# A graph layer with attention and experts: where the last node tiles' work stands in the queues

## The chip, the cores and the metric

The kernel runs on one core of a Trainium2 chip. The metric is the device time of one execution in microseconds (us). Each number of "time" is a median of several executions; the profile is one execution, taken by the hardware profiler.

## The reference

The input is 6250 nodes of 256 features and 206,250 directed edges (src, dst). With `xn = layernorm(x)` the layer computes three things.

```
# 1. graph attention, 4 heads of 64 features
h  = xn @ W;  el = h @ Wl.T;  er = h @ Wr.T
e  = exp(leaky_relu(el[src] + er[dst], 0.2))          # one weight per edge and head
g  = elu(segment_sum(e * h[dst], src) / segment_sum(e, src) + b)
# 2. linear attention with 4 memory entries, 4 heads of 32
q, k, v = split(rmsnorm(xn) @ w_qkv)
q = softmax(q over the features of a head);  k = softmax(k over all nodes)
a = rmsnorm(((k.T @ v) applied to q) @ w_out + b_out) + xn
# 3. mixture of 8 experts, the best 2 of each node
x2 = x + g + a
t  = layernorm(x2)
y  = t + sum over experts of combine[:, e] * (gelu(t @ w1[e] + b1[e]) @ w2[e] + b2[e])
out = x2 + y
```

## The kernel before

**Tiles.** The nodes lie in 49 tiles of 128 (the last one has 106). The edges are 1612 columns of 128.

**Sorting and projecting.** Four node tiles at a time are normalised and multiplied with all weights of the first two parts (`project`); the rows that the edges will need go to a table in DRAM. Between these groups, and behind them, `sort_batch` runs 51 times. It takes 32 columns of edges and puts them in order of their pairs of node tiles: a one-hot `ob` (L381), counts `n_ps` (L389) and their scan `inc` (L393), the sums `ahead` (L406), the ranks' sums `r_ps` in PSUM (matmuls L413 and L414), `rank` from them (L421 and L427), `rank2` on ACT (L433), the values `rv` (L438), the one-hot `ohp` (L442), and 32 matmuls into `g_ps` (L448), which ACT copies to `grid` (L453). Pool `sps` has one buffer of each PSUM tile; `rv` and `ohp` have two. `context` computes the keys' softmax and `k.T @ v` between the last batches.

**Packing and gathering.** `pack(q)` makes from the grid the ordered list of edges of two node tiles (on DVE the products `rc` L914 and one-hots `ohc` L907, `ohp` L919; on PE `s_ps` L924). For each of the two tiles `gather` then issues 35 indirect DMAs on GpSimd's queue (POOL, L952). Each brings 128 rows of 69 numbers into one column of `xe`, of which there are three buffers.

**Node tiles.** The loop at L1051 goes over blocks of up to GT = 4 node tiles. A node tile `b` does `weights` (scores `z`: the reduction L998, the addition L1002, which is the first to need the gathered rows; the exponential L1005; the copy L1006) and then four times `sums` (the product `ohw` on DVE, L1014, and some 24 matmuls into `a_ps`, L1021), `look` for the next tile (its one-hots and `e_ps`), in odd tiles a `pack`, and `some_more`. ACT then copies the sums (`a_s`, L1067), PE transposes them (L1070), and `heads` divides by the weights' sums (L817 to L819).

**What is done beside it.** `todo` is a queue of generators. The first is `attention`: three steps for each of 13 groups, 39 in all. Each finished block adds `finish_steps`: `front` (elu, sum and layernorm, L665 to L709), `route` (the best two experts, L712 to L757), and nine steps over the experts, in each of which `hidden` computes one expert's two halves (`h_ps` L764, Gelu L772) and `result` adds the expert before it (`y_ps` L780, `x` L784); 11 steps in all. `hps` has one buffer, so `h_ps` is one PSUM bank. When the attention has ended, the experts' weights are loaded (`open_experts`). `some_more()` runs one step; `some_more(c)` runs the c-th part of what is still in the queue. In blocks of four each quarter of a tile calls it once; in smaller blocks the queue is spread over the quarters that are left in the block. The 49 tiles are cut into nine blocks of four and then 3, 2, 2, 2, 1, 1, 1, 1, which end at tiles 38, 40, 42, 44, 45, 46, 47 and 48.

**Order.** The framework puts the instructions of each engine in an order of its own from the order written down, its estimates of when operands are there, and the dependencies; on the chip each engine then runs its queue in that order. A `NoSync` dependency fixes an order on one engine and waits for nothing. `keep_in_program_order` ties an instruction behind the one written just before it on its engine. Should more edges than there are columns belong to a tile, `flag` is set and a slow path recomputes everything.

Of the kernel before, what the change touches and what calls it, by code (L numbers as in the profile page):

```python
# [17 lines left out]
P = 128  # L18
GT = 4
# [16 lines left out]
def tile_gps_layer(  # L36
# [43 lines left out]
    NB = NQ + NQ % 2  # L80
    BB = min(CB, 512 // NB)
    assert BW % BB == 0 and U == 2
    TW = H + FO + 1
    VW = HF + H
    CS = CPT // S
# [6 lines left out]

    groups = [(t0, min(GT, NT - t0)) for t0 in range(0, NT, GT)]

    sizes = []
    while sum(sizes) < NT:
        sizes.append(min(GT, -(-(NT - sum(sizes)) // (GT + 1))))
    blocks = [(sum(sizes[:i]), n) for i, n in enumerate(sizes)]

    cp = ctx.enter_context(tc.tile_pool(name="const", bufs=1))  # L100
# [263 lines left out]
    def sort_batch(t):  # L364
# [41 lines left out]
        nc.vector.tensor_tensor(  # L406
            pairs(ahead[:, :w]), two(inc[:, :w], NB // 2), row(delta, NB // 2), op=OP.mult
        )
        r_ps = sps.tile([P, BW // BB, 512], F32, name="r_ps")
        for i, a in enumerate(range(0, w, BB)):  # L410
            z = min(w, a + BB)
            part = r_ps[:, i, :(z - a) * NB]
# [20 lines left out]
        nc.scalar.activation(  # L433
            rank2[:, :w], rank[:, :w, None].to_broadcast([P, w, 2]), AF.Identity, bias=less_own
        )
        rv = sw.tile([P, BW, 2, NB], F16, name="rv")
        for i, v in enumerate((va, vb)):
            nc.vector.tensor_tensor(  # L438
                pairs(rv[:, :w, i, :]), pairs(ob[:, :w]), two(v[:, cs], NB // 2), op=OP.mult
            )  # L440
        ohp = sw.tile([P, BW, P], F16, name="ohp")
        nc.vector.tensor_tensor(  # L442
            pairs(ohp[:, :w]), two(rank2[:, :w], P // 2), row(iota_h, P // 2), op=OP.is_equal
        )
# [206 lines left out]
        W["fw"] = fx.enter_context(tc.tile_pool(name="ffnw", bufs=1, side="right"))  # L651


    def finish_steps(hps, yps, x2, t0, n, rows_left, gb):

        w = n * P
        held = {}
# [101 lines left out]
        def hidden(e, f):  # L759
            if f == 0:  # L760
                held[e] = fw.tile([P, FC, GT * P], F32, name="hT", bufs=2)
            h_ps = hps.tile([P, GT * P], F32, name="h_ps")
            for c in range(DC):
                nc.tensor.matmul(  # L764
                    h_ps[:, :w],
                    lhsT=w1s[:, e, c, f * P:(f + 1) * P],
                    rhs=held["tokT"][:, c, :w],
                    start=(c == 0),
                    stop=(c == DC - 1),
                )  # L770
            k = e * FC + f
            nc.scalar.activation(  # L772
                held[e][:, f, :w], h_ps[:, :w], AF.Gelu, bias=b1s[:, k:k + 1]
            )

        def result(e, js):
            for j in js:
                y_ps = yps.tile([P, D], F32, name="y_ps")
                for f in range(FC):
                    nc.tensor.matmul(  # L780
                        y_ps, lhsT=held[e][:, f, j * P:(j + 1) * P], rhs=w2s[:, e, f, :],
                        start=(f == 0), stop=(f == FC - 1),
                    )
                nc.vector.scalar_tensor_tensor(  # L784
                    x2[:, j, :], y_ps, held["comb"][:, j, e:e + 1], x2[:, j, :],
                    op0=OP.mult, op1=OP.add,
                )

        def store():
            full = n if rows_left is None else n - 1  # L790
# [69 lines left out]
    def pack(q):  # L860
# [88 lines left out]
    def gather(dst_x):  # L949
        xe = gw.tile([P, CPT, TW], F32, name="xe", bufs=3)  # L950
        for c in range(CPT):
            nc.gpsimd.indirect_dma_start(  # L952
                out=xe[:, c, :],
                out_offset=None,
                in_=table,
                in_offset=bass.IndirectOffsetOnAxis(ap=dst_x[:, c:c + 1], axis=0),
            )
        return xe
# [34 lines left out]
                    start=False, stop=(g0 + g == GC - 1),  # L993
                )

    def weights(xe, e_ps):
        z = gw.tile([P, CPT, H], F32, name="z")
        nc.vector.tensor_reduce(  # L998
            z, e_ps[:, 1:].rearrange("p c i h -> p c h i"), axis=AX.X, op=OP.add
        )  # L1000

        tc.keep_in_program_order(nc.vector.tensor_add(z, z, xe[:, :, :H]))  # L1002
        nc.vector.scalar_tensor_tensor(z, z, 0.2, z, op0=OP.mult, op1=OP.max)
        ew = gw.tile([P, CPT, H], F32, name="ew")
        nc.scalar.activation(ew, z, AF.Exp)  # L1005
        nc.vector.tensor_copy(ew_s, ew)  # L1006


    def sums(i, oh, xe, a_ps):
        g0, g1 = CELLS[i]  # L1010
        n = g1 - g0
        c0 = i * CS - 1 + g0
        ohw = gw.tile([P, GC, H, SN], F32, name="ohw")
        nc.vector.tensor_tensor(  # L1014
            ohw[:, :n],
            oh[:, g0:g1, i, None, :].to_broadcast([P, n, H, SN]),
            ew_s[:, c0:c0 + n, :, None].to_broadcast([P, n, H, SN]),
            op=OP.mult,
        )
        for c in range(c0, c0 + n):  # L1020
            nc.tensor.matmul(  # L1021
                a_ps[:, i].rearrange("f h n -> f (h n)"),
                lhsT=xe[:, c, H:],
                rhs=ohw[:, c - c0].rearrange("p h n -> p (h n)"),
                start=(c == c0), stop=(c == c0 + n - 1),
            )
# [24 lines left out]
    for t0, n in blocks:  # L1051
        x2 = gw.tile([P, GT, D], F32, name="x2", bufs=3)
        for j in range(n):
            b = t0 + j
            xe, _ = ready.pop(b)
            oh, e_ps = seen.pop(b)
            weights(xe, e_ps)
            a_ps = pa.tile([FO + 1, S, H, SN], F32, name="a_ps")
            for k in range(S):
                sums(k, oh, xe, a_ps)  # L1060
# [13 lines left out]
            heads(x2[:, j, :], hd_ps[:, :, :FO], hd_ps[:, :, FO])  # L1074
        rows_left = None if (t0 + n) * P <= N else last
        todo.append([finish_steps(hps, yps, x2, t0, n, rows_left, gb_s), NX + 3])

    seen_n = count[0:1].rearrange("p q u s -> p (q u) s")[:, :NT]
    away = cp.tile([1, NT, S], F32, name="away")
# [137 lines left out]
```

## Time and profile before

| what | before |
|---|---|
| time, median of 3 runs | 2762.55 us (2759.88 to 2763.56) |
| time of the profiled execution | 2760.09 us |
| its span, first to last instruction | 2758.0 us |
| mean granted TensorE clock | 0.82 |
| busy: PE, DVE, ACT, POOL | 76%, 70%, 27%, 61% |
| first gather issued, last gather's end | 443.9 us, 2635.4 us |

PE is TensorE's matmuls, PEld its weight loads, DVE VectorE, ACT ScalarE, POOL GpSimd, SP the queue of plain transfers. A row of a group reads: line, engine, operation, what it writes and reads, how often, then the busy time in us, the mean duration in ns, and the time that its engine stood idle just before it with what ended that. A row of waits reads: who waited for whom, us in total, times, longest. A row of stretches reads: from and to, length, busy time of each engine with its number of instructions, granted clock, share of the DMA engines, GB/s. A line of the timeline reads: start, duration, engine, line and operation, and in brackets the idle time before it and what ended it. All in us from the start of the span.

### The profile page before, as it was taken

The page shows a single profiled execution, that of the slowest core. Times are in us where ns is not written, and L with a number is a line of the kernel's source. Part 1 is how long each engine was busy: PE and PEld are TensorE (multiplying, and loading weights), DVE is VectorE, ACT ScalarE, POOL GpSimd, SP SyncE. Part 2 cuts the span into 40 slices and gives each one's busy share as a digit, 9 for nine tenths or more (in the row PEclk, how much of TensorE's full clock was granted, in tenths as well). Part 3 has the DMA queues.
Part 4 walks back from the last instruction along what each step waited for, and adds up shares of the span by engine and source line. Part 5 has one row for each costly group of instructions (what it writes and reads, how often), then busy time and mean ns, then how long its engine had stood idle before and what let it go on. Part 6 is the DMA issues. An engine that isn't in the chain of part 4 may idle for free.

```text
span 2758.0 us, 39898 instructions
## 1 busy us (share of the span) xinstructions
PE 2108.4 (76%) x15539; PEld 1584.8 (57%) x15539; DVE 1939.9 (70%) x3992; ACT 753.6 (27%) x1691; POOL 1688.5 (61%) x1779
## 2 busy tenths in 40 slices
PE   6888664556465498969899889596895988887987
PEld 3555442445354367656667667465675666666774
DVE  6877977668487668775879568765776676876742
ACT  4655311112231132213223222021221322232333
POOL 1000204777777777777677777777777777777610
PEclk9878665666677599979999889698796999888887
DMA  2110200222222422121212212212122221221110
GB/s 70 33 30 25 20 1 15 44 59 58 58 59 52 109 36 44 29 44 29 41 29 44 37 36 37 36 29 36 36 29 36 34 40 29 38 37 34 33 15 5
DMA packets 106775, 103.96 MB, mean 38 GB/s; under 512 B 42822, under 2 KB 78884, under 8 KB 106580
## 3 DMA queue, kind: packets, MB, share of 16 engines
q0 software_dynamic: 54880, 60.70, 14.6%
q1 hardware_dynamic: 50004, 39.75, 5.1%
q8 instruction: 124, 2.03, 0.3%
q10 hardware_dynamic: 1696, 0.89, 0.1%
q14 instruction: 71, 0.58, 0.1%
HBM read 86.57 MB, written 14.65 MB: 37 GB/s over the span
## 4 chain that ended last, share of the span: by engine, by line
POOL 29%; PE 26%; DVE 15%; issue 14%; ACT 2%; DMA 2%; DVEq 0%; ACTq 0%; POOLq 0%
POOL xe L952 28%; PE a_ps L1021 8%; PE h_ps L764 7%; PE y_ps L780 6%; DVE rc L914 4%; DVE ohp L919 3%; DVE ohc L907 2%; DMA xe<-table,dst_x 2%; PE y_ps L704 1%; DVE ohw L1014 1%; PE y_ps L755 1%; PE s_ps L924 1%; DVE x L784 1%; POOL kv L492 1%; PE y_ps L699 1%
## 5 line engine op out<-in xcount | busy, mean ns | idle before, releaser
L952 POOL DMA_INDIRECT xe<-table,dst_x x1715 | 1654.5, 965 | 632.7 <-issue 604.4
L1021 PE MATMUL a_ps<-ohw,xe 128*65 128x128 f32 x4410 | 552.1, 283 | 16.3 <-DVE ohw L1014 12.7
L1021 PEld LDWEIGHTS a_ps<-ohw,xe 128*65 128x65 f32 x4410 | 518.2, 144 | 50.9 <-DVE ohw L1014 19.2
L924 PE MATMUL s_ps<-rc,ohp 128*128 128x144 f16 x2525 | 257.4, 275 | 279.7 <-DVE ohp L919 279.6
L764 PE MATMUL h_ps<-tokT,w1s 128*128 128x512 f32 (+3 forms) x1088 | 431.3, 515 | 47.5 <-ACT hT L772 45.4
L924 PEld LDWEIGHTS <-ohp 128*128 128x128 f16 x2525 | 224.7, 121 | 342.9 <-DVE ohp L919 321.5
L780 PE MATMUL y_ps<-w2s,hT 128*128 128x256 f32 x1568 | 405.6, 390 | 0.0
L784 DVE SCALAR_TENSOR_TENSOR x<-y_ps,comb,x 128x256 f32<-128x256 f32 x392 | 189.0, 484 | 230.3 <-PE y_ps L780 230.0
L1014 DVE TENSOR_TENSOR ohw<-oh,bank 128x1280 f32<-128x1280 bf16 x196 | 323.4, 1650 | 32.3 <-PE a_ps L1021 30.8
L780 PEld LDWEIGHTS y_ps<-w2s,hT 128*128 128x128 f32 x1568 | 285.0, 193 | 66.3 <-issue 28.7
L772 ACT ACTIVATE hT<-h_ps,b1s 128x512 f32<-128x512 f32 (+3 forms) x272 | 154.4, 568 | 555.4 <-PE h_ps L764 412.1
L764 PEld LDWEIGHTS h_ps<-tokT,w1s 128*128 128x128 f32 x1088 | 193.6, 205 | 151.3 <-ACT hT L772 79.5
L914 DVE TENSOR_TENSOR rc<-ohc,bank 128x1152 f16<-128x1152 f16 (+1 forms) x350 | 228.0, 693 | 4.5 <-PE s_ps L924 0.7
L919 DVE TENSOR_TENSOR ohp<-to,bank 128x2048 f16<-128x2048 f16 (+1 forms) x175 | 195.1, 1115 | 0.0
L981 ACT COPY ohT<-t_ps 128x768 bf16<-128x768 bf16 x98 | 78.2, 798 | 319.0 <-PE t_ps L977 318.9
L1002 DVE TENSOR_TENSOR z<-z,xe 128x140 f32<-128x140 f32 x49 | 15.0, 307 | 210.6 <-DMA xe<-table,dst_x 202.5
L350 POOL COPY el<-tab 128x16 f32<-128x16 f32 (+1 forms) x13 | 3.5, 267 | 260.7 <-ACT tab L349 260.7
L907 DVE TENSOR_TENSOR ohc<-to,bank 128x1152 f16<-128x1152 f16 (+1 forms) x175 | 121.2, 692 | 0.4 <-ACT to L896 0.4
L442 DVE TENSOR_TENSOR ohp<-rank,iota_h 128x4096 f16<-128x4096 f16 (+1 forms) x51 | 116.1, 2277 | 6.3 <-ACT rank L433 6.0
L342 PE MATMUL pr<-wcat,xT 128*128 128x456 f32 x196 | 109.9, 691 | 5.9 <-ACT xT L339 5.9
L1067 ACT COPY a_s<-a_ps 65x512 f32<-65x512 f32 x49 | 28.4, 580 | 280.6 <-PE a_ps L1021 280.4
L448 PEld LDWEIGHTS <-ohp 128*128 128x128 f16 x1612 | 62.3, 109 | 56.4 <-DVE ohp L442 45.6
(269 smaller groups left out, 2483.9 us busy)
## 6 DMA issues: line engine op xcount, KB each, us to landing
xe<-table,dst_x POOLq DMA_INDIRECT x1715, 2.5
xt<-in_x_dram SPq DMA_DIRECT2D x24, 512.0 KB, 3.9
base_y<-xt SPq DMA_DIRECT2D x12, 512.0 KB
yt<-base_y SPq DMA_DIRECT2D x9, 512.0 KB, 4.4
out_dram<-x SPq DMA_DIRECT2D x9, 512.0 KB
w1s<-in_L_ffn_w_dram SPq DMA_DIRECT2D x8, 256.0 KB
w2s<-in_L_ffn_w_dram SPq DMA_DIRECT2D x8, 256.0 KB, 5.3
table<-tab SPq DMA_DIRECT2D x12, 138.0 KB
```

What stands on the lines that cost most here:

```text
L442: nc.vector.tensor_tensor(pairs(ohp[:, :w]), two(rank2[:, :w], P // 2), row(iota_h, P // 2), op=OP.is_equal)
L764: nc.tensor.matmul(h_ps[:, :w], lhsT=w1s[:, e, c, f * P:(f + 1) * P], rhs=held["tokT"][:, c, :w], start=(c == 0), stop=(c == DC - 1),)
L772: nc.scalar.activation(held[e][:, f, :w], h_ps[:, :w], AF.Gelu, bias=b1s[:, k:k + 1])
L780: nc.tensor.matmul(y_ps, lhsT=held[e][:, f, j * P:(j + 1) * P], rhs=w2s[:, e, f, :], start=(f == 0), stop=(f == FC - 1),)
L784: nc.vector.scalar_tensor_tensor(x2[:, j, :], y_ps, held["comb"][:, j, e:e + 1], x2[:, j, :], op0=OP.mult, op1=OP.add,)
L907: nc.vector.tensor_tensor(pairs(ohc[:, :m]), twos(to[:, 0, t0:t0 + m], U * CW // 2), iota_2[:, :, :U * CW // 2].to_broadcast([P, m, U * CW ...
L914: nc.vector.tensor_tensor(pairs(rc[:, :m, i, :]), pairs(ohc[:, :m]), twos(edges_q[:, t0:t0 + m, i, :], U * CW // 2), op=OP.mult,)
L919: nc.vector.tensor_tensor(pairs(ohp[:, :m]), twos(to[:, 1, t0:t0 + m], P // 2), iota_2.to_broadcast([P, m, P // 2, 2]), op=OP.is_equal,)
L924: nc.tensor.matmul(flat(s_ps), lhsT=ohp[:, t - t0, :], rhs=flat(rc[:, t - t0]), start=(t == 0), stop=(t == NBT - 1),)
L952: nc.gpsimd.indirect_dma_start(out=xe[:, c, :], out_offset=None, in_=table, in_offset=bass.IndirectOffsetOnAxis(ap=dst_x[:, c:c + 1], axis=0),
L1014: nc.vector.tensor_tensor(ohw[:, :n], oh[:, g0:g1, i, None, :].to_broadcast([P, n, H, SN]), ew_s[:, c0:c0 + n, :, None].to_broadcast([P, n ...
L1021: nc.tensor.matmul(a_ps[:, i].rearrange("f h n -> f (h n)"), lhsT=xe[:, c, H:], rhs=ohw[:, c - c0].rearrange("p h n -> p (h n)"), start=(c ...
```

## The change

It has five parts.

- In the sort, `r_ps` has two buffers (two more PSUM banks), and `rv` and `ohp` have three for two.
- As long as the attention runs, the quarters 1 and 3 of a tile call `some_more` once more: six steps a tile for four.
- The blocks are nine of four and then 3, 3, 3, 2, 1, 1; they end at tiles 38, 41, 44, 46, 47 and 48.
- In a block of one tile, everything in the queue is run ahead of the tile's `weights`, and nothing between its quarters. The addition L1002 of that tile is tied on DVE behind the last four results of the experts (L784). In these blocks the second half of `hidden` takes its bank from the pool `pl`, whose tile `s_ps` the packs use.
- The last node tile gathers 30 columns for 35 (its expected number of edges plus four times its root, in columns), and computes with 30.

```diff
+    mean = NE * last / N
+    CPL = min(CPT, -(-int(mean + 4 * mean ** 0.5) // P))
...
-    sizes = []
-    while sum(sizes) < NT:
-        sizes.append(min(GT, -(-(NT - sum(sizes)) // (GT + 1))))
+    sizes, rest = [], NT
+    for n in (1, 1, 2, 3, 3, 3):
+        if rest > n:
+            sizes.insert(0, n)
+            rest -= n
+    sizes = [GT] * (rest // GT) + ([rest % GT] if rest % GT else []) + sizes
...
-        r_ps = sps.tile([P, BW // BB, 512], F32, name="r_ps")
+        r_ps = sps.tile([P, BW // BB, 512], F32, name="r_ps", bufs=2)
...
-        rv = sw.tile([P, BW, 2, NB], F16, name="rv")
+        rv = sw.tile([P, BW, 2, NB], F16, name="rv", bufs=3)
...
-        ohp = sw.tile([P, BW, P], F16, name="ohp")
+        ohp = sw.tile([P, BW, P], F16, name="ohp", bufs=3)
...
+    results = []
+    def finish_steps(hps, yps, x2, t0, n, rows_left, gb, more=None):
...
-            h_ps = hps.tile([P, GT * P], F32, name="h_ps")
+            if more is not None and f % 2:
+                h_ps = more.tile([P, P], F32, name="s_ps")
+            else:
+                h_ps = hps.tile([P, GT * P], F32, name="h_ps")
...
-                nc.vector.scalar_tensor_tensor(
+                results.append(nc.vector.scalar_tensor_tensor(
                     x2[:, j, :], y_ps, held["comb"][:, j, e:e + 1], x2[:, j, :],
                     op0=OP.mult, op1=OP.add,
-                )
+                ))
...
-            ready[q * U + u] = (gather(dst_x[:, u * CW:u * CW + CPT]), loc)
+            ready[q * U + u] = (gather(dst_x[:, u * CW:], columns(q * U + u)), loc)
+
+    def columns(b):
+        return CPT if b < NT - 1 else CPL
...
-        for c in range(CPT):
+        for c in range(n):
...
-    def weights(xe, e_ps):
+    def weights(xe, e_ps, n, behind):
...
-        tc.keep_in_program_order(nc.vector.tensor_add(z, z, xe[:, :, :H]))
+        ins = nc.vector.tensor_add(z, z, xe[:, :n, :H])
+        tc.keep_in_program_order(ins)
+        for other in behind:
+            tc.add_manual_dep(
+                ins.ins, other.ins.name,
+                mybir.DependencyInfo(mybir.DependencyClass.NoSync, mybir.DependencyReason.DATA),
+            )
...
         g0, g1 = CELLS[i]
+        g1 = min(g1, end - i * CS + 1)
...
-            weights(xe, e_ps)
+            if n == 1:
+                some_more(1)
+
+            weights(xe, e_ps, columns(b), results[-GT:] if n == 1 else [])
...
-                some_more(None if n == GT else (n - j) * S - k)
+                if n > 1:
+                    some_more(None if n == GT else (n - j) * S - k)
+
+                if k % 2 and "fw" not in W:
+                    some_more()
...
+        more = pl if n == 1 else None
+        todo.append([finish_steps(hps, yps, x2, t0, n, rows_left, gb_s, more), NX + 3])
...
+    most = float((NT - 1) % U * CW * P + CPL * P)
+    nc.vector.tensor_single_scalar(
+        away[:, NT - 1:, S - 1], seen_n[:, NT - 1:, S - 1], most, op=OP.is_gt
+    )
```

More of the change, by code (lines that the diff above doesn't have):

```diff
@@ L651, in open_experts @@
         W["fw"] = fx.enter_context(tc.tile_pool(name="ffnw", bufs=1, side="right"))
-    def finish_steps(hps, yps, x2, t0, n, rows_left, gb):
+    results = []
+    def finish_steps(hps, yps, x2, t0, n, rows_left, gb, more=None):
         w = n * P
@@ L946, in pack, with gather @@
                 )
-            ready[q * U + u] = (gather(dst_x[:, u * CW:u * CW + CPT]), loc)
-    def gather(dst_x):
+            ready[q * U + u] = (gather(dst_x[:, u * CW:], columns(q * U + u)), loc)
+    def columns(b):
+        return CPT if b < NT - 1 else CPL
+    def gather(dst_x, n):
         xe = gw.tile([P, CPT, TW], F32, name="xe", bufs=3)
-        for c in range(CPT):
+        for c in range(n):
             nc.gpsimd.indirect_dma_start(
@@ L994, in look, with sums @@
                 )
-    def weights(xe, e_ps):
-        z = gw.tile([P, CPT, H], F32, name="z")
+    def weights(xe, e_ps, n, behind):
+        z = gw.tile([P, CPT, H], F32, name="z")[:, :n]
         nc.vector.tensor_reduce(
-            z, e_ps[:, 1:].rearrange("p c i h -> p c h i"), axis=AX.X, op=OP.add
+            z, e_ps[:, 1:1 + n].rearrange("p c i h -> p c h i"), axis=AX.X, op=OP.add
         )
-        tc.keep_in_program_order(nc.vector.tensor_add(z, z, xe[:, :, :H]))
+        ins = nc.vector.tensor_add(z, z, xe[:, :n, :H])
[5 more added lines that the diff above has]
+            )
         nc.vector.scalar_tensor_tensor(z, z, 0.2, z, op0=OP.mult, op1=OP.max)
-        ew = gw.tile([P, CPT, H], F32, name="ew")
+        ew = gw.tile([P, CPT, H], F32, name="ew")[:, :n]
         nc.scalar.activation(ew, z, AF.Exp)
-        nc.vector.tensor_copy(ew_s, ew)
-    def sums(i, oh, xe, a_ps):
+        nc.vector.tensor_copy(ew_s[:, :n], ew)
+    def sums(i, oh, xe, a_ps, end):
         g0, g1 = CELLS[i]
+        g1 = min(g1, end - i * CS + 1)
         n = g1 - g0
@@ L1056, in tile_gps_layer @@
             oh, e_ps = seen.pop(b)
-            weights(xe, e_ps)
+            if n == 1:
+                some_more(1)
+            weights(xe, e_ps, columns(b), results[-GT:] if n == 1 else [])
             a_ps = pa.tile([FO + 1, S, H, SN], F32, name="a_ps")
             for k in range(S):
-                sums(k, oh, xe, a_ps)
+                sums(k, oh, xe, a_ps, columns(b))
                 if b + 1 < NT:
@@ L1075, in tile_gps_layer @@
         rows_left = None if (t0 + n) * P <= N else last
-        todo.append([finish_steps(hps, yps, x2, t0, n, rows_left, gb_s), NX + 3])
+        more = pl if n == 1 else None
+        todo.append([finish_steps(hps, yps, x2, t0, n, rows_left, gb_s, more), NX + 3])
     seen_n = count[0:1].rearrange("p q u s -> p (q u) s")[:, :NT]
```

## The prediction

> **What bounds the kernel now.** I read the page first: the chain that ended last, then the gather's row, then busy time by stretch.
>
> ```profile
> span 2758.0 us, 39898 instructions
> ...
> POOL 29%; PE 26%; DVE 15%; issue 14%; ACT 2%; DMA 2%; DVEq 0%; ACTq 0%; POOLq 0%
> ...
> L952 POOL DMA_INDIRECT xe<-table,dst_x x1715 | 1654.5, 965 | 632.7 <-issue 604.4
> ```
>
> 1715 gathers (49 node tiles of 35 columns) take 965 ns each and POOL idles about 0.3 us between two: 1.25 us a column, 44.5 us a tile. By the gather's own timeline the first is issued at 443.9 and the last at 2634.5. So there are three parts: sorting and projecting (0 to 443.9), a gather-paced middle (to 2635.4), and a tail of 117.6 us behind the last landing (2640.4). POOL waits noticeably three times, for a tile buffer that the sums still hold (three buffers): 7.5 us before tile 20, 2.6 before tile 44, and here before tile 48:
>
> ```profile
> 2592.04 0.94 POOL L952 DMA_INDIRECT xe<-table,dst_x  x1 [5.46 <-PE a_ps L1021]
> ```
>
> Who sets the end is seen in DVE's timeline. The last time that anything but a backlog of computation is waited for is tile 46's score addition (L1002):
>
> ```profile
> 2545.51 0.30 DVE L1002 TENSOR_TENSOR z<-z,xe 128x140 f32<-128x140 f32 x1 [10.47 <-DMA xe<-table,dst_x]
> ```
>
> DVE stands still for 10.47 us with tile 45's sums, a pack and routing behind it. From there 212.5 us of work follow to the end; tiles 47 and 48 are added at 2609.3 and 2644.3, 20 and 4 us after their landings, with DVE busy until then. The end thus hangs on the landing of tile 46 plus a backlog, not on the landing of tile 48. The stretches of the tail:
>
> ```profile
> 2640.40:2691.30 50.90, 44.08 (x272) 36.46 (x271) 23.91 (x60) 17.74 (x34) 0.00 (x0) 0.87 0.03 9
> 2691.30:2718.20 26.90, 21.75 (x104) 14.90 (x103) 7.74 (x32) 11.37 (x23) 0.00 (x0) 0.87 0.00 1
> 2718.20:2731.80 13.60, 5.45 (x18) 3.91 (x19) 7.65 (x36) 5.86 (x10) 0.00 (x0) 0.56 0.03 10
> 2731.80:2752.00 20.20, 18.93 (x88) 12.68 (x87) 3.87 (x8) 5.51 (x15) 0.00 (x0) 0.87 0.01 2
> 2752.00:2758.00 6.00, 0.00 (x0) 0.00 (x0) 0.00 (x0) 0.00 (x0) 0.00 (x0) 0.67 0.09 28
> ```
>
> Columns: length, then PE, PEld, DVE, ACT, POOL busy, clock, DMA. They hold tile 46's experts around the sums of tile 48, then tile 47's experts, tile 48's front and routing, its experts, its store.
>
> **Second bank and third buffers in the sort.** Stretches of the sort, and its waits from 24 to 408.7:
>
> ```profile
> 65.00:284.00 219.00, 195.65 (x2299) 115.70 (x2295) 171.01 (x280) 132.34 (x512) 3.86 (x22) 0.82 0.11 32
> 284.00:340.00 56.00, 35.60 (x480) 23.19 (x478) 53.68 (x59) 14.78 (x42) 11.10 (x9) 0.60 0.28 7
> 340.00:408.70 68.70, 46.44 (x669) 33.19 (x670) 52.76 (x74) 12.40 (x49) 8.21 (x7) 0.65 0.01 1
> ```
>
> ```profile
> DVE rv L438 <- PE g_ps L448: 43.8, 32, 4.6
> PE g_ps L448 <- DVE ohp L442: 36.5, 25, 4.4
> PE r_ps L413 <- DVE rank L421: 17.3, 17, 10.8
> ```
>
> The third rv and ohp buffers remove the 43.8 us row, the second bank the 17.3 us row. But 284 to 340 has 2.3 us of DVE idle: nothing to win. From 65 to 284 PE is busy 195.65 of 219: at most 23 us, and with projections between the batches I take 6. From 340 on a batch takes 6.92 us for 6.1 of DVE work, because rank, ohp, the grouping matmuls and the next r_ps follow one another; an rv done earlier lets `ahead` go before ohp: 0.8 us for each of some 8 batches, 6 us. Sum 12; ends 0 (PE's order keeps it) and 23 + 7 = 30. All of it is on the path, as the first pack follows the last batch. A different order could also lose; the nearest row, the 4.5 us that a batch at 344 waited for ACT, bounds that at +5.
>
> **Attention, six steps a tile for four.** Its 39 steps end at tile 6.5, not 9.75. A group of three costs DVE about 9.6 us by its rows, so two more steps add 6.4 us a tile to about 30 of 44.5: hidden by the gather, and DVE idles 115.4 us for tile landings between 500 and 1000. If that cover is gone, POOL waits: tile 5's sums end 7.2 us before its buffer is wanted again, tile 11's 5.7. I take 0, bound 6. SP gets the same loads and stores earlier; the experts' 4 MB land earlier, while gathers kept their 1.25 us in the same traffic before. In return the experts have caught up with the gather by about tile 12, not 22 to 24. The 7.5 us before tile 20 fell into that backlog (tile 17's sums ended 98 us after its landing; later groups of four stay under 87): I take it as removed, and of the 2.6 before tile 44 half, less 2 for new waits: -7, ends -10 and +6.
>
> **Last blocks 3, 3, 3, 2, 1, 1 for 3, 2, 2, 2, 1, 1, 1, 1.** PE's cost of an expert is 6.9 us for four tiles (1.72 for four h_ps and 1.73 for eight y_ps matmuls, twice, in the chain), 3.5 for two, by proportion 5.2 for three, 2.4 for one (DVE's results 2.45 us apart). Eight experts: 14 us a tile in blocks, 19.5 single; two singles fewer give back 11 us of PE. But the block of tiles 42 to 44 comes after tile 44, so behind the landing of tile 46 there are experts of seven tiles, not six: 42 + 28 + 2 x 19.5 = 109 for 28 + 4 x 19.5 = 106. PE's work is even; what differs is the order.
>
> **Experts in front of single tiles.** All of block 45-46 goes before tile 47's weights, all of tile 47's before tile 48's, and L1002 is tied behind the last four results on DVE. Queued behind that addition are the exponential on ACT, four multiplications on DVE and 90 matmuls on PE. So the end becomes a chain, which I price from the rows of tile 48, which ran alone:
> - tiles 45-46: front and routing 13.6 + 2.9 to the first result + 3.6 for wider rows, then 7 x 3.5: 45
> - sums of 47: add, exponential with its table load, copy, first product 4.4, 90 matmuls at 0.116 = 10.5, copy and transposes 1.4, and the look at tile 48: 17.5
> - tile 47: 33.8 (13.6 + 20.2), less 2 for the second hidden bank = 32. PE's start-to-start of a half step is 1.2 us while its pure streams are 0.9; half of 16 x 0.3; end 0 also possible
> - sums of 48: 15.7, with 85 matmuls
> - tile 48: 32, store 6
> Sum 148 from the heads of tile 46. In the trace its sums were copied at 2614.8, 73 us after the landing. With three-tile experts at 2 and 1 steps a call I expect 72 to 80 us again and the heads there, not at 2636.8 behind another block: 2618. End 2618 + 148 = 2766, +8 on 2758. Ends: heads 50 us after the landing (the shorter lags of even tiles are 45 to 65) give 2740, -18; heads at 2629, with everything of 42-44 in front and no idle PE filled, gives 2777, +19, and 6 more without the second hidden bank: +25.
>
> The Trainium skill, "TensorE: Matmul & The Clock Gate", section "What's actually happening", speaks against this part: an idle stretch returns PE to half rate and about 3.4 us of work are needed to leave it. The trace has it: clock 0.56 in 2718.20 to 2731.80, and the first h_ps fours behind it take 1.06 to 1.09 us, later ones 0.71. By the page's figure two more such stretches would cost an estimated 2 x 1.7 = 3.4 us; in my sum they are inside the 33.8 us of the rows.
>
> **Last tile 30 columns.** Five gathers of 1.25 us: 6.2 us less POOL time, five matmuls and a shorter product. As the end hangs on tile 46, the 6.2 us, and the 5.46 before tile 48, shorten a wait that is not last: 0, except 0.6 in the sums (counted). If the backlog were gone, 6.2.
>
> **Sum.** 2758 - 12 - 7 + 8 = 2747 span; the profiled run took 2760.09 for 2758.0, so 2749; it lay 2.5 below the median 2762.55: 2752.
>
> **Rivals.**
> - The backlog dissolves. If attention turning faster and three-tile blocks bring the heads of tile 46 to 50 us behind its landing or less, the tail gives -18, then 2758 - 12 - 7 - 18 = 2721, 2726 as a median. For it: PE is busy only 27.3 of the 43 us from 2517 to 2560. Against: the even tiles with four steps lag 65 in every group of four, and DVE's 10.47 us wait has the same order behind it.
> - The chain costs more (slower). One mechanism: L1002 tied behind the results puts front, routing and experts of 45-46 and 47 end to end with the sums, where before the fronts of 46 and 47 ran beside sums. At +25, with the sort at 4 and the waits at 3, 2758 + 25 - 7 = 2776, median 2780. It decides once the heads of tile 46 come later than 2629: then it takes the 19 us that the other parts give. For it: 117.6 us of the old tail have 27 of PE idle, my chain has about 55 (two more fronts, routings and weight steps). Against: before, the same queue put tile 48's heads 26 us behind its copy.
> - The banks do nothing, as PE's order and not the buffers sets the batches: sort 0, waits -7, tail +8: 2759, median 2764, no change.
>
> **Numbers.** Forecast 0.45, backlog dissolves 0.18, chain 0.22, banks nothing 0.15. My own case spans 2742 to 2764 by the middle of its bounds. No change, within 0.2% (5.5 us, about what a measurement of this kernel can tell), is 2757 to 2768: a fifth of my case and nearly all of the last. Faster 0.36 + 0.18 + 0.01 = 0.55, same 0.09 + 0.12 = 0.21, slower 0.24. Range 2724 to 2780.
>
> **What the next profile would show.** Right: first gather near 432; no wait of POOL before tile 20; attention over by tile 7; DVE's L1002 of tiles 47 and 48 directly behind an L784; from the heads of tile 46 to the end near 148 us. Wrong: a first gather at 443 (banks useless); L1002 of tile 48 waiting for its landing (backlog gone, and the 30 columns count); POOL waits before tiles 4 to 8 (attention too dense).

## The result, and the profile after

| | before | after |
|---|---|---|
| time, median | 2763.06 us (2759.88 to 2765.48) | 2802.03 us (2801.74 to 2806.38) |
| ratio, 95% interval | | 1.0145 (1.0128 to 1.0163) |
| span of the profiled execution | 2758.0 us | 2799.9 us |
| first gather issued | 443.9 us | 460.4 us |
| from there to the last gather of tile 46 | 2098.6 us | 2124.7 us |
| from there to the end | 215.5 us | 214.8 us |

The changed kernel is slower by 39 us, outside the predicted range. The three stretches of the table add up to the spans: +16.5 in the sort, +26.1 while the gather sets the pace, -0.7 in the tail. The whole loss is in the two parts that I had put down as gains.

The page of the changed kernel first: the span, the chain that ended last by engines, and the gather's row.

```profile
span 2799.9 us, 39518 instructions
...
PE 30%; POOL 24%; DVE 18%; issue 12%; ACT 2%; DMA 2%; DVEq 0%; POOLq 0%; ACTq 0%
...
L966 POOL DMA_INDIRECT xe<-table,dst_x x1710 | 1653.0, 967 | 644.7 <-issue 598.7
```

The gather (now L966) still takes 967 ns, five are gone, and yet POOL idles 12 us more. Its share of the chain that ended last falls from 29% to 24% while PE's and DVE's rise: for longer than before, something other than the gather set the end. POOL's waits say where (who waited for whom, us in total, times, longest): first the kernel before, from the first gather to tile 46, then the changed kernel from 820 to 1290. The first line of POOL's timeline behind the longest wait follows.

```profile
POOL xe L952 <- PE a_ps L1021: 10.1, 2, 7.5
```

```profile
POOL xe L966 <- PE a_ps L1042: 33.5, 4, 14.8
```

```profile
1113.73 0.95 POOL L966 DMA_INDIRECT xe<-table,dst_x  x1 [14.75 <-PE a_ps L1042]
```

Four waits for a tile buffer that the sums of three tiles earlier still hold: 6.0, 7.5, 14.8 and 5.2 us before tiles 10, 12, 14 and 16. None of a microsecond or more comes later. Before, such waits were 10.1 us up to tile 46, and both of them (7.5 us before tile 20, 2.6 before tile 44) are gone. The waits make 23.4 of the 26.1 us; another 3.2 are gathers that each took 2 ns longer.

The sort's own waits: two rows of DVE in the kernel before (24 to 409 us), then DVE from 24 to 425 us in the changed one, and its stretch from 65 to 284 (length, then PE, PEld, DVE, ACT, POOL busy, clock, DMA):

```profile
DVE ob L381 <- PE r_ps L413: 13.6, 10, 3.8
DVE rank L421 <- PE r_ps L414: 9.3, 14, 1.4
```

```profile
DVE ob L387 <- PE r_ps L419: 52.0, 25, 4.3
DVE rank L427 <- PE r_ps L420: 27.1, 17, 2.2
...
DVE ohp L448 <- ACT rank L439: 8.0, 12, 5.6
```

```profile
65.00:284.00 219.00, 191.35 (x2112) 108.60 (x2109) 156.54 (x255) 118.53 (x464) 2.73 (x18) 0.75 0.09 27
```

The 43.8 us row of `rv` is gone, as the third buffers were to make it. In its place `ob` waits 52.0 us where it had waited 13.6, and `rank` 27.1 where it had waited 9.3. DVE's idle time from 24 to 408.7 rises from 80.8 to 98.7 us, by about what the first gather is late. PE is busy almost as long as before (191.35 for 195.65) but gets through 2112 matmuls where it had got through 2299, at a mean granted clock of 0.75 for 0.82. The page's busy share alone would not have told it.

DVE's timeline shows the new wait, one of 25:

```profile
151.94 0.57 DVE L387 TENSOR_TENSOR ob<-bid,iota_h 128x832 f16<-128x832 f16 x1
152.62 0.59 DVE L444 TENSOR_TENSOR rv<-ob,va 128x832 f16<-128x832 f16 x1
153.13 0.58 DVE L444 TENSOR_TENSOR rv<-ob,vb 128x832 f16<-128x832 f16 x1
158.03 0.59 DVE L387 TENSOR_TENSOR ob<-bid,iota_h 128x832 f16<-128x832 f16 x1 [4.32 <-PE r_ps L419]
158.54 1.02 DVE L427 TENSOR_REDUCE rank<-r_ps 128x32 f32<-128x832 f32 x1
```

Two `ob` stand in DVE's queue with no `rank` between them. `ob` has two buffers, and the matmul L419 that reads the older one stands on PE behind four projection matmuls that end at about 157.8. So DVE waits 4.32 us at the second `ob`, with `rank` queued behind it. No slow clock makes this wait: PE is busy throughout, and the granted clock (the column behind the five engines) is 1.00:

```profile
153.80:158.00 4.20, 4.20 (x44) 2.36 (x42) 0.00 (x0) 4.08 (x19) 0.00 (x0) 1.00 0.02 4
```

In the kernel before, the same stretch has `rank` (151.98) and `ahead` (153.21) behind the `ob` of 151.47, and the next `ob` only at 161.24.

The tail did much of what was written down for it. L1016 is the score addition (L1002 before) in DVE's timeline:

```profile
2588.06 0.31 DVE L1016 TENSOR_TENSOR z<-z,xe 128x140 f32<-128x140 f32 x1 [4.95 <-DMA xe<-table,dst_x]
```

Tile 46's addition is again the last that waits for a landing. Those of tiles 47 and 48 start at 2705.0 and 2749.9 without a wait; the latter's rows had landed about 81 us before.

In the runs e5 to e11, e13 to e16, e18 and e19 the kernel before itself took 4376 to 4393 us, with engines that stand still during gathers (last section), so their times are not compared with the others and only what comes ahead of the first gather is used.

### The profile page after: what moved, and what is told of

Same layout as the page of the kernel before. It is cut to its first block, busy times and chain, and to the rows that moved or that the text cites. A ratio compares the mean times of both kernels' runs of the same rounds, so it can differ in the third digit from the quotient of the medians.

```text
span 2799.9 us, 39518 instructions
## 1 busy us (share of the span) xinstructions
PE 2134.1 (76%) x15401; PEld 1592.2 (57%) x15401; DVE 1935.8 (69%) x3941; ACT 724.2 (26%) x1638; POOL 1686.8 (60%) x1774
## 4 chain that ended last, share of the span: by engine, by line
PE 30%; POOL 24%; DVE 18%; issue 12%; ACT 2%; DMA 2%; DVEq 0%; POOLq 0%; ACTq 0%
POOL xe L966 23%; PE a_ps L1042 10%; PE h_ps L775 7%; PE y_ps L791 7%; DVE rc L925 5%; DVE ohp L930 4%; DVE ohc L918 2%; DMA xe<-table,dst_x 2%; PE y_ps L712 1%; PE y_ps L763 1%; DVE ohw L1035 1%; PE s_ps L935 1%; DVE inc L889 1%; DVE x L795 1%; PE y_ps L707 1%
## 5 line engine op out<-in xcount | busy, mean ns | idle before, releaser
L966 POOL DMA_INDIRECT xe<-table,dst_x x1710 | 1653.0, 967 | 644.7 <-issue 598.7
L1042 PEld LDWEIGHTS a_ps<-ohw,xe 128*65 128x65 f32 x4400 | 526.7, 147 | 83.9 <-issue 40.6
L775 PE MATMUL h_ps<-tokT,w1s 128*128 128x512 f32 (+3 forms) x896 | 407.4, 574 | 21.4 <-ACT hT L783 21.4
L935 PEld LDWEIGHTS <-ohp 128*128 128x128 f16 x2525 | 225.0, 122 | 329.7 <-DVE ohp L930 310.0
L791 PE MATMUL y_ps<-w2s,hT 128*128 128x256 f32 x1568 | 395.5, 388 | 1.8 <-DVE x L795 1.8
L783 ACT ACTIVATE hT<-h_ps,b1s 128x512 f32<-128x512 f32 (+3 forms) x224 | 140.4, 627 | 526.8 <-PE h_ps L775 381.1
L775 PEld LDWEIGHTS h_ps<-tokT,w1s 128*128 128x128 f32 x896 | 165.9, 204 | 114.1 <-issue 64.4
L1016 DVE TENSOR_TENSOR z<-z,xe 128x140 f32<-128x140 f32 (+1 forms) x49 | 14.8, 302 | 171.3 <-DMA xe<-table,dst_x 168.4
L454 PE MATMUL g_ps<-rv,ohp 128*128 128x52 f16 x1612 | 67.7, 207 | 44.2 <-DVE ohp L448 43.8
```

Source lines behind the costliest of these rows:

```text
L775: nc.tensor.matmul(h_ps[:, :w], lhsT=w1s[:, e, c, f * P:(f + 1) * P], rhs=held["tokT"][:, c, :w], start=(c == 0), stop=(c == DC - 1),)
L783: nc.scalar.activation(held[e][:, f, :w], h_ps[:, :w], AF.Gelu, bias=b1s[:, k:k + 1])
L791: nc.tensor.matmul(y_ps, lhsT=held[e][:, f, j * P:(j + 1) * P], rhs=w2s[:, e, f, :], start=(f == 0), stop=(f == FC - 1),)
L935: nc.tensor.matmul(flat(s_ps), lhsT=ohp[:, t - t0, :], rhs=flat(rc[:, t - t0]), start=(t == 0), stop=(t == NBT - 1),)
L966: nc.gpsimd.indirect_dma_start(out=xe[:, c, :], out_offset=None, in_=table, in_offset=bass.IndirectOffsetOnAxis(ap=dst_x[:, c:c + 1], axis=0),
L1042: nc.tensor.matmul(a_ps[:, i].rearrange("f h n -> f (h n)"), lhsT=xe[:, c, H:], rhs=ohw[:, c - c0].rearrange("p h n -> p (h n)"), start=(c ...
```

## The experiments

My theory after seeing the trace: the parts are independent and add up, the sort's third buffers cost 17 us by way of `ob`, and attention's six steps cost 23 by way of a backlog that makes POOL wait. The rivals: the second bank itself disturbs PE's order; the waits come from the packs of the odd tiles and not from the backlog; the tail hides a loss.

**One part at a time (e1 to e4, same chip; before 2764.07 us).** e1 is the kernel before with all three edits of the sort, e4 with the bank alone:

```diff
-        r_ps = sps.tile([P, BW // BB, 512], F32, name="r_ps")
+        r_ps = sps.tile([P, BW // BB, 512], F32, name="r_ps", bufs=2)   # e1 and e4
...
-        rv = sw.tile([P, BW, 2, NB], F16, name="rv")
+        rv = sw.tile([P, BW, 2, NB], F16, name="rv", bufs=3)            # e1 alone
...
-        ohp = sw.tile([P, BW, P], F16, name="ohp")
+        ohp = sw.tile([P, BW, P], F16, name="ohp", bufs=3)              # e1 alone
```

> The kernel before with the second bank for r_ps and the third buffers for rv and ohp, nothing else. Theory A (the sort's buffers alone make the sort slower, by putting DVE's one-hot ob ahead of where PE can follow): first gather near 460 instead of 444, time +13 to +18, near 2778. Rival B (the late first gather comes from another part of the change, as the order of the whole program is made anew): first gather 430 to 446, time 2750 to 2765.

> The kernel before with only the second bank for r_ps. If the second bank lets ob run ahead and block DVE, first gather near 455 to 460 and time +10 to +16. If rv and ohp do it, first gather within 4 us of 444 and time within 5 us of the kernel before. If each is harmless alone and only both together cost, the same.

e1: 2780.84 us, ratio 1.0066 (1.0050 to 1.0081), first gather at 462.6. e4: 2760.43 us, 0.9986 (0.9977 to 0.9996), first gather at 439.1. The bank is worth some 4 us; what costs is the third buffers. DVE's waits in the sort of e1, and then of e4:

```profile
DVE ob L381 <- PE r_ps L413: 53.6, 25, 4.3
DVE rank L421 <- PE r_ps L414: 27.1, 17, 2.2
```

```profile
DVE rv L438 <- PE g_ps L448: 42.6, 31, 3.0
DVE ob L381 <- PE r_ps L413: 12.2, 10, 2.4
```

With the bank alone the old wait of `rv` stays; with the third buffers it turns into that of `ob`.

e2 is the kernel before with attention's two extra calls, and nothing else:

```diff
                 some_more(None if n == GT else (n - j) * S - k)
+                if k % 2 and "fw" not in W:
+                    some_more()
```

> The kernel before with six attention steps a tile, nothing else. Theory A (the earlier experts run into a denser backlog and POOL waits for tile buffers before tiles 10 to 16): first gather at 444, 15 to 30 us of POOL waits for sums between tiles 10 and 20, time +8 to +25. Rival B (the waits come from the late sort or from the new blocks, attention is hidden as predicted): POOL waits under 10 in all, time 2750 to 2765.

2787.52 us, ratio 1.0082 (1.0066 to 1.0097), first gather at 447.4: POOL waits 4.8, 6.9, 15.0 and 4.4 us before tiles 10, 12, 14 and 16, the pattern of the changed kernel, and 2.4 and 4.5 us before tiles 42 and 44. Its row from 820 to 1290:

```profile
POOL xe L952 <- PE a_ps L1021: 31.1, 4, 15.0
```

e3 is the changed kernel without the sort's buffers and the extra calls: blocks of 3, 3, 3, 2, 1, 1, experts in front of single tiles, 30 columns.

> The changed kernel without the sort's buffers and without the extra attention steps: only the blocks, the experts in front of single tiles with their second bank, and the 30 columns. Theory A (the end is even: it ends 214 to 216 us behind the last gather of tile 46 in both profiles): 2755 to 2765. Rival B (the serial chain at the end costs, as the slower rival of the prediction said): 2770 to 2785.

2761.86 us, ratio 0.9993 (0.9984 to 1.0002): no change that can be told. The last gather ends at 2622.0, 13 us earlier than before, and the addition of tile 48 starts at 2707.4, 83 us after its landing: what POOL saves at the end reaches nobody.

The parts add up. Against 2764.07 they are +16.8, +23.4 and -2.2, in sum 38.0, and the whole change is +39.0. Within their intervals (some 4 us either way for e1 and e2) nothing is lost between the parts.

**What in the sort costs (e5, e6, e9).** e5 has the third buffers of `rv` and `ohp` without the bank. e6, and e9 once more, have the bank and three buffers of `rv` and of `ob`, while `ohp` keeps two:

```diff
-        ob = sw.tile([P, BW, NB], F16, name="ob")
+        ob = sw.tile([P, BW, NB], F16, name="ob", bufs=3)                # e6 and e9; r_ps 2, rv 3
```

> The kernel before with the third buffers for rv and ohp, without the second bank. The bank alone brought the first gather from 443.9 to 439.1; all three together put it to 462.6. Theory A (the third buffers do the harm: the order puts work of later batches ahead on DVE, where it then waits): first gather 455 to 470, time +10 to +25. Rival B (only bank and buffers together do harm): first gather 436 to 446, time within 5 us of the kernel before.

> The kernel before with the second bank, a third buffer for rv, and a third buffer for the one-hot ob instead of ohp. In the changed kernel DVE waited 52 us for ob's buffer (r_ps matmuls of two batches before), against 13.6 before. Theory A (that buffer is what DVE runs into once the others no longer stop it): the wait of ob falls under 10 us, first gather 425 to 440, time -5 to -20. Rival B (PE's order decides, more buffers only make DVE wait elsewhere): first gather 440 to 465, time 0 to +20.

> The kernel before with two banks for r_ps, three buffers of rv and three of ob; ohp keeps two. Theory: in the changed kernel ob of a later batch stands ahead on DVE and waits there until the r_ps matmul of two batches earlier has let go of one of its two buffers (52.0 us of DVE idle before ob); with three buffers of ob that wait is gone and the first gather starts near 422, 22 us before that of the kernel before, so that the time falls by 15 to 25 us, to 2739 to 2749. Rival: the gather is not what the gained time reaches, since node tiles later wait for attention or experts; then the time falls by less than 10 us.

DVE's waits in us from 24 us to the end of the batches (390 to 425 us, by kernel), and the first gather:

| kernel | `rv` | `ob` | `rank` | first gather |
|---|---|---|---|---|
| before | 43.8 | 13.6 | 9.3 | 443.9 |
| e4: bank | 42.6 | 12.2 | 7.4 | 439.1 |
| e5: `rv`, `ohp` 3 | none | 49.8 | 29.5 | 460.9 |
| e1: bank, `rv`, `ohp` 3 | none | 53.6 | 27.1 | 462.6 |
| after | none | 52.0 | 27.1 | 460.4 |
| e9: bank, `rv`, `ob` 3 | 22.7 | 8.5 | 14.5 | 417.2 |

e6 has its first gather at 421.7. The same gain that I had hoped for from the third buffers is there, and twice as large, once `ob` has one too:

```profile
DVE rv L438 <- PE g_ps L448: 22.7, 11, 4.1
DVE rank L421 <- PE r_ps L414: 14.5, 17, 2.1
DVE ob L381 <- PE r_ps L413: 8.5, 6, 3.1
```

These three lines are e9's waits of DVE up to 390 us. That e5 loses without the bank rules out the rival that the bank disturbs PE. e1 and e9 differ in two things, `ob`'s third buffer and `ohp`'s return to two. The row that vanishes is `ob`'s, which speaks for the first; a run with `ob` and `ohp` both at two beside three of `rv` was not made, so the share of each stays open. The times of e5, e6 and e9 (4404.79, 4356.54 and 4366.61 us) are not read.

**Why POOL waits in the backlog (e2's trace; e7, e8, e10, e11, e15, e16).** e2's windows show tile 11, whose sums were copied 108 us after its landing (columns as above):

```profile
1024.60:1074.10 49.50, 49.28 (x218) 33.46 (x216) 22.85 (x55) 10.46 (x16) 37.62 (x40) 1.00 0.19 28
1074.10:1095.00 20.90, 13.50 (x127) 10.39 (x126) 20.90 (x33) 1.97 (x2) 8.88 (x10) 1.00 0.13 18
```

For 49.5 us PE does experts back to back while DVE is half idle; then for 20.9 us DVE does the pack, without a pause, while PE waits for it. The two stand one behind the other, 70.4 us in a tile for which the gather gives 44.5. PE's timeline in the second of them has the last experts' `y_ps` between the pack's groups, and still 1.3 us of waiting for DVE at each:

```profile
1077.74 1.18 PE L924 MATMUL s_ps<-rc,ohp 128*128 128x144 f16 x16 [1.29 <-DVE ohp L919]
1078.80 1.13 PE L780 MATMUL y_ps<-w2s,hT 128*128 128x256 f32 x4
1081.26 1.17 PE L924 MATMUL s_ps<-rc,ohp 128*128 128x144 f16 x16 [1.33 <-DVE ohp L919]
```

Counting the Gelus between two copies of sums gives 15 half experts in tile 11, none in 12, 13 in tile 13 and 3 in 14. A block's queue is 11 steps; at four steps a tile it lasts 2.75 tiles, and the order piles the experts into every second tile, the one that also packs. In the kernel before, sets of that size lie in tiles 11, 17 and 19 (15, 15 and 12). What differs is how late such a tile starts: by the DMA's packets tile 11's addition began there 1 us after its landing and its sums were copied 80 us after it; tile 17's began 6 us late, its sums came after 94, and that one made tile 20 wait. In e2, where the attention ends at tile 6.5 and the sets follow each other from tile 7, tile 11 began 20 us late and tile 13 26. The remedy to try is a lower pace in one kind of tile:

```diff
-                some_more(None if n == GT else (n - j) * S - k)
+                if n < GT or "fw" not in W or b % 2 == 0 or k < 2:       # e7, e10, e15: odd tiles thinned
+                    some_more(None if n == GT else (n - j) * S - k)
+                if k % 2 and "fw" not in W:
+                    some_more()
```

e8, e11 and e16 have `b % 2 == 1` in its place, which thins the even tiles.

> Six attention steps a tile as in e2_attn, and behind the attention, in blocks of four, odd tiles (those with a pack) run two expert steps for four, even tiles four. Three steps a tile still keep up (11 steps come with four tiles). Theory A (density: with four steps a tile in a backlog the queues need more than the gather's 44.5 us a tile, so the sums fall behind until POOL waits): the waits of 31 us before tiles 10 to 16 go, time 2755 to 2768. Theory B (it is the meeting of a full set of experts with a pack in odd tiles): the same here. Rival C (the early start of the experts itself, their weights' loads or the front, costs): waits of 15 us and more stay, 2775 to 2790.

> As e7_thin_odd, but with the even tiles thinned to two steps and four in the odd ones, beside the packs. Theory A (density): the waits go as in e7_thin_odd, time 2755 to 2768. Theory B (meeting with the packs): waits of 15 us or more between tiles 10 and 20 stay, time 2775 to 2795.

> The kernel before with six attention steps a tile, and after the attention only two expert steps in an odd tile of a block of four (the tiles that also hold a pack). Theory 'an odd tile is too full': POOL waits before tiles 12 and 14 fall from some 22 us to below 5, and the time from 2787 to 2755 to 2770. Rival 'the backlog as a whole, not the odd tiles': the waits before tiles 10 to 16 stay above 15 us, time 2775 to 2790.

> The same with the even tiles thinned to two expert steps and the odd ones left at four. Theory 'an odd tile is too full': the waits before tiles 12 and 14 stay, some 20 us, time 2775 to 2790. Rival 'density of the backlog, wherever it lies': the waits go as with the odd tiles thinned, time 2755 to 2770.

> The kernel before with six attention steps a tile, and after the attention only two expert steps in an odd tile of a block of four (the tiles that also hold a pack). Theory 'an odd tile is too full': POOL's waits before tiles 12 and 14 fall from some 22 us to below 5, and the time from 2787 to 2755 to 2770. Rival 'the backlog as a whole, not the odd tiles': the waits before tiles 10 to 16 stay above 15 us, time 2775 to 2790.

> The same with the even tiles thinned to two expert steps and the odd ones left at four. Theory 'an odd tile is too full': the waits before tiles 12 and 14 stay, some 20 us, time 2775 to 2790. Rival 'density of the backlog, wherever it lies': the waits go as with the odd tiles thinned, time 2755 to 2770.

None of the six decides it. The odd tiles thinned took 4392.89, 4392.26 and 4387.32 us, the even ones 4344.59, 4338.87 and 4346.40, beside 4383.66, 4389.88 and 4376.16 for the kernel before; every tile's sums came over 100 us after their landing already with tile 0, and POOL waited before nearly every tile, whatever the pace. The two edits also differ less than their texts: the half experts of tiles 11 to 14 fall in sets of 8, 4, 4 and 0 in e15 and of 9, 3, 4 and 0 in e16, so that the pair hardly varies what it was to test. Why the even ones are 41 to 53 us faster in these runs is not explained.

**The repaired kernel (e17, then e13, e14, e18, e19).** e17 is the whole changed kernel with `ob` at three buffers, `ohp` at two, and the odd tiles of blocks of four thinned:

```diff
-        ob = sw.tile([P, BW, NB], F16, name="ob")
+        ob = sw.tile([P, BW, NB], F16, name="ob", bufs=3)
...
-        ohp = sw.tile([P, BW, P], F16, name="ohp", bufs=3)
+        ohp = sw.tile([P, BW, P], F16, name="ohp")
...
-                if n > 1:
+                if n > 1 and (n < GT or "fw" not in W or b % 2 == 0 or k < 2):
                     some_more(None if n == GT else (n - j) * S - k)
```

> The whole changed kernel with two edits: in the sort ob has three buffers and ohp two, and after the attention an odd tile of a block of four takes two expert steps for four. Theory (the full sets in odd tiles make POOL wait; the sort's limit was ob): first gather near 422, no more than 10 us of waits before tiles 10 to 20, time 2730 to 2745, faster than both kernels. Rival (the thinner backlog only lasts longer and the waits come later): waits of 15 us and more in sum, time 2750 to 2775.

2724.68 us (2724.53 to 2725.44) beside 2762.43 for the kernel before: ratio 0.9858 (0.9838 to 0.9877), faster than both kernels and below the 2730 to 2745 that were expected. Its page, and POOL's waits between the first gather and tile 46:

```profile
span 2722.7 us, 39488 instructions
...
POOL 30%; PE 24%; DVE 15%; issue 14%; DMA 3%; ACT 1%; DVEq 0%; SPq 0%; POOLq 0%; ACTq 0%
...
L966 POOL DMA_INDIRECT xe<-table,dst_x x1710 | 1646.1, 963 | 611.7 <-issue 592.2
```

```profile
POOL xe L966 <- PE a_ps L1042: 3.7, 3, 3.1
```

POOL is first in the chain again. Its waits of a microsecond or more are down from 33.5 us to one of 3.1, and the sets in tiles 11 to 14 are now 8, 4, 4 and 0 half experts. Against the changed kernel the three stretches give -42.6 (first gather at 417.8), -36.3 and +1.7, in sum the 77.2 us between the spans; against the kernel before they give -26.1, -10.2 and +1.0. So the sort's gain (first gather at 417.2 in e9, which has the same edits in the sort) reaches the end in full, which settles the question that e9 had left. The middle's gain is put down to the thinning and not to the sort, since e1, with a sort 18.6 us later, has a middle of 2098.5 us for 2098.6.

e13, and e14 and e19 once more, have the end's parts and the sort of e9, with attention's four steps as before. e18 is e17 with the even tiles thinned for the odd ones.

> The changed kernel's blocks, experts in front of single tiles and 30 columns, with attention's four steps as before, and in the sort two banks of r_ps, three buffers of rv and three of ob (ohp two). Theory (the parts add up): first gather near 422, -22; end parts -2; one wait of about 8 us before tile 20: 2738 to 2746, faster than both kernels. Rival (the earlier gather lands in front of a backlog that is no earlier): 2750 to 2762.

> The changed kernel's blocks, experts in front of single tiles and 30 columns, with attention's four steps as before, and in the sort two banks of r_ps, three buffers of rv and three of ob (ohp two). Theory (the parts add up): first gather near 422, -22; end parts -2; one wait of about 8 us before tile 20: 2738 to 2746, faster than both kernels. Rival (the earlier gather runs into a backlog that is no earlier, and POOL waits more): 2750 to 2762.

> The kernel of e17 with the even tiles thinned to two expert steps and the odd ones left at four. Theory 'the odd tile is too full' (a pack and a full set of expert steps): POOL waits 15 us or more before tiles 10 to 16, time 2738 to 2760. Rival 'any thinning does it' (the half experts fall in smaller sets either way): waits below 8 us, time within 4 us of e17's 2724.7.

> The changed kernel's blocks, experts in front of single tiles and 30 columns, with attention's four steps as before, and in the sort two banks of r_ps, three buffers of rv and of ob (ohp two). If the parts add up: first gather near 420 (-25), end parts -2, a wait of about 8 us before tile 20: 2733 to 2742. Rival (the attention's six steps with thinner odd tiles give nothing, the tail takes up the wait): 2722 to 2728 as in e17.

Their first gathers start at 421.9, 420.9, 417.3 and 425.8 us: the sort's gain held in each. Their times (4353.02, 4330.04, 4311.25 and 4342.70 us) are not read. Two things stay open: whether e17 needs the odd tiles thinned or any thinning would do (the sets of e15 and e16 are nearly the same), and whether it needs attention's six steps at all. The middle stretch, where both would show, is worth 10 of its 35 us.

## Why the prediction was wrong

- **Sort: -12 expected, bounds -30 and +5; measured +16.5.** The step that failed is "the third rv and ohp buffers remove the 43.8 us row, the second bank the 17.3 us row", and behind it the bound of a lost order. I treated waits as amounts to be taken away. Of the 17.3 us row, 10.8 were one wait at 300 us, inside the stretch that the prediction had set aside, and e4 with the second bank has it as well (11.3 us, there put down to `ahead`). The third buffers let the order run ahead on DVE until the next tile with two buffers stopped it, and that was `ob`, whose 13.6 us wait stood in the same list of waits. The bound of +5 took one 4.5 us wait of one batch as the price of a worse order; a wait that belongs to the order returns with each batch, here 25 times with up to 4.3 us. `ob`'s ten waits before were 1.4 us each; the same for half of the 51 batches would have been 35 us, 21 more than its 13.6, and the sort's measured +16.5 would have lain inside.
- **Attention: -7 expected, bounds -10 and +6; measured 23.4 us more waits in the changed kernel, and +23.4 us in e2's time.** That the two agree to the tenth is chance: e2's profiled run has 27.9 us more waits. The waits of 7.5 and 2.6 us that were to go did go in the changed kernel; four new ones came, 33.5 us in all. "Two more steps add 6.4 us a tile to about 30 of 44.5: hidden" was right for the tiles where the attention runs: no wait falls before tiles 4 to 8. What failed is "the experts have caught up with the gather by about tile 12". They had by tile 16, and on the way two full sets fell into tiles 11 and 13, which also started late. I had costed the steps that move and not the pace at which the queue behind them then runs; tile 17's lag, which I did name (98 us; 94 by the DMA's packets, as tile 46's 73 are 70), was the same thing at a later place.
- **Tail: +8 expected; measured -0.7, alone 0.9993.** The kind was right: heads of tile 46 behind its landing, then one chain. The gather's end to the heads took 72.3 us (75.5 by my times). From the heads to the end took 142.5 for 148: tile 46's block 47.6 (45), sums of 47 16.9 (17.5), tile 47 28.0 (32), sums of 48 15.8 (15.7), tile 48 with its store 34.2 (38). The two single tiles were each 4 us shorter than priced: I had taken 2 us for the hidden second bank, half of the 16 x 0.3 us between the half steps, and it gave about the whole. PE's timeline of tile 47 has one expert in 1.76 us without a gap between its streams, `s_ps` being the borrowed bank:

```profile
2739.69 0.61 PE L775 MATMUL h_ps<-tokT,w1s 128*128 128x128 f32 x4
2740.14 0.61 PE L775 MATMUL s_ps<-tokT,w1s 128*128 128x128 f32 x4
2740.58 1.03 PE L791 MATMUL y_ps<-w2s,hT 128*128 128x256 f32 x4
2741.45 0.61 PE L775 MATMUL h_ps<-tokT,w1s 128*128 128x128 f32 x4
```

  Behind the front the same fours are slower, 1.06 to 1.22 us in four of them and 1.91 for the first `y_ps`: 3.0 us more for one front in this timeline. The granted clock is 0.50 in this stretch and 1.00 in the next:

```profile
2724.40:2738.00 13.60, 8.79 (x30) 6.89 (x31) 5.79 (x30) 5.92 (x11) 0.00 (x0) 0.50 0.03 10
2738.10:2751.60 13.50, 11.40 (x76) 10.33 (x75) 5.00 (x12) 6.00 (x14) 0.00 (x0) 1.00 0.03 10
```

  The slow fours go on for 9.4 us, from 2728.62 to 2738.0, with a pause of 2.2 us for the routing between them. The Trainium skill ("TensorE: Matmul & The Clock Gate", "What's actually happening") has an idle stretch return PE to half rate, and about 3.4 us of work lead out of it; the prediction's estimate from it was 1.7 us for a front. The half rate agrees, but it lasts longer here, so that the measured price is higher.
- **30 columns: 0 expected, and none seen.** The last gather ends earlier and tile 48's addition starts 81 us after its landing (83 in e3). No run has the 30 columns alone.
- **The rivals.** Slower had a chance of 0.24, but for a chain in the tail that in fact came out even. "The banks do nothing" is true of the bank (e4, -3.6 us in time) and not of the buffers. No rival had the sort or the attention ending on the slower side, although the text gave both a positive bound; these two bounds, +5 and +6, were the prediction's real error. Together they became +40.

## What to carry to other kernels

In this sort third buffers moved the queue's stop to the next tile that had two: before giving one, read the list of waits for all tiles of the stage, and give it to the tile whose wait would come next. When a step is moved out of a stretch, count what the queue behind it will do per tile at the new pace, and look for two bounds (here PE's experts and DVE's pack) that come to lie one behind the other in one tile. A worse order can cost its wait in every round, not once: here 25 times.

## What the runs showed of the hardware

PE's busy time told little of its work. From 65 to 284 us PE was busy 190.6 to 195.7 us in the kernels before, after, e1, e4 and e17, yet it got through 2299, 2112, 2122, 2253 and 2349 matmuls, at mean granted clocks of 0.82, 0.75, 0.76, 0.81 and 0.84 (the mix of matmuls is not quite the same in the five). Whether the mean clock fell because of DVE's waits or the reverse was not separated.

In e9 PE, DVE and ACT stood still while gathers went out. Three windows of it, columns as above: the gather's first half, its second half, and the time behind it.

```profile
2057.10:2079.70 22.60, 16.41 (x84) 12.17 (x83) 9.03 (x14) 3.00 (x4) 17.11 (x19) 0.92 0.15 27
2079.70:2106.50 26.80, 0.59 (x1) 0.00 (x0) 0.00 (x1) 0.00 (x0) 16.02 (x17) 0.51 0.16 24
2106.50:2124.40 17.90, 16.98 (x105) 14.24 (x105) 13.68 (x30) 9.92 (x12) 0.00 (x1) 0.87 0.16 52
```

In the middle row POOL issues its gathers at the usual pace, and PE, DVE and ACT do one matmul and next to nothing else in 26.8 us, at a clock of 0.51; all three start again within 1 us of 2106.5, 7 us behind the last gather. What they waited for is not in the trace. One thing beside it is: of the instruction fetches of 8 or 16 KB between the first and the last gather, 12 of 138 start 20 to 45 us behind a tile's first gather in e9, and 71 of 140 in the kernel before. Whether the engines stood still for want of instructions, or fetched none because they stood still, stays open.
